# Turning the rows of an attention input by transposing transfers instead of on TensorE

## The chip, the cores and the metric

The kernel runs on one core of one Trainium2 chip. The metric is the device time of one execution in microseconds, the median over the runs shown. A profile of one execution stands beside it; all rows quoted here are from that profile or from queries of its trace. TensorE multiplies matrices out of SBUF into PSUM, ScalarE (ACT) and VectorE (DVE) do element-wise work, GpSimd (POOL) issues the indirect transfers here, and SyncE (SP) issues the plain ones. Each engine works through its own instructions in order.

## The reference

The input has 16 batches of 512 features by 1024 tokens, and a mask of zeros and ones by token. One attention layer of 8 heads is added to the input; queries, keys and values are the same projection:

```python
xt = jnp.transpose(x, (0, 2, 1))                       # x: (16, 512, 1024)
q = xt @ Wq.T
qh = q.reshape(B, T, NH, dk).transpose(0, 2, 1, 3)     # NH = 8, dk = 64
scores = scale * jnp.einsum('bhqd,bhkd->bhqk', qh, qh)
cmask = mask[:, None, None, :]
rmask = mask[:, None, :, None]
logits = (scores * cmask + (1.0 - cmask) * NEG) * rmask
attn = jax.nn.softmax(logits, axis=-1)
ctx = jnp.einsum('bhqk,bhkd->bhqd', attn, qh)
out = ctx.transpose(0, 2, 1, 3).reshape(B, T, D) @ Wo.T
return x + jnp.transpose(out, (0, 2, 1))
```

About half of the tokens of a batch are masked. A masked query gets all logits zero, so its attention is the plain mean over all tokens; an unmasked query attends only to unmasked tokens.

## The kernel before, in words

The kernel keeps only the unmasked ("active") tokens of a batch: up to 544 for batches 0 to 4, 528 for 5 to 13 and 512 for 14 and 15 (`self.wide`); batches 2 to 15 are ordered by their number of active tokens. Index lists are computed on the chip, and the rows of active tokens are gathered by indirect transfers into tiles of 128 tokens by 512 features (`gather`, tag `xa`, 13 buffers; the 32 or 16 rows beyond 512 go to `xt`, one buffer).

Method `xt` (line 476) brings them into the layout that the projection wants, features on partitions: four transposes per tile on TensorE against the identity (L486), into PSUM, and then `xsplit` makes two half-precision parts of the result: ScalarE writes the rounded value times 256 to `xh` (L444), VectorE the remainder to `xl` (L445). `xh` and `xl` exist once, 4 blocks of 546 columns each; column A, behind the active tokens, takes the mean over all tokens. The mean comes from a plain load of the batch (`load_all`, tag `xm`) that ScalarE sums (L425).

`query` (L513) multiplies these by the weights, three half-precision products per block of features, for four blocks e of outputs and two halves g of the columns. `qsplit` splits the result again and spreads it over partitions by four SP transfers (`xx`, L540 to L543). `value` brings it back to tokens on partitions; `scores` (L701) forms two heads' scores for 128 keys, ScalarE takes the exponential (L705, tag `p`, 12 buffers); `attend` (L726) multiplies by the values. The remainder of the tokens beyond 512 (`i` is None, L676, L680) is packed for four heads, split by VectorE and spread by SP transfers (`pt`, L692, L693), and taken up by L730. `recip_rows` sends the reciprocals of the sums through DRAM (`rd`, L769; `rb`, L773); `norm` applies them and splits the context; `project` (L817) multiplies by the output weights, VectorE adds the input row (L822), and an indirect transfer writes the rows out (`scatter`, L901).

The masked tokens' rows get one vector per batch, the projected mean: `late` gathers them (tag `xi`, 8 buffers), `rest` adds the vector `ub` (tag `ub`, 3 buffers; L888) and writes the row out. They are handled one to three batches after their own.

The loop `run` goes over 16 batches in 18 steps. While batch b's scores are formed, a list `m` of units for batch b+1 (the transposes, queries, values) and for batch b-1 (norm, project) is worked off in proportion to given costs. At the start of `m` stand the units of `xt` for batch b+1; query e=0 follows at once. Gathers for batch b+2 come late in iteration b. Transfers on POOL are posted to two lines and issued one a step; each waits for the matmul traced before it. The engines' final orders are laid out at build time by a planner that sorts by priority and estimated readiness; `high_priority(offset=HPO)` (300) puts an instruction ahead of its place, `behind` orders instructions of one engine. A tile under a tag waits for one of its buffers to be free.

```python
m = sums + x[:2] + second + x[2:4] + (value(b, 3) if b else []) + rows + x[4:] + pk(b, 1)
```

Batch 0 and the first parts of batch 1 are worked before the loop.

Of the kernel before, what the change touches and what calls it, by code (L numbers as in the profile page):

```python
# [22 lines left out]
H = 8  # L23
DK = 64
NP = H // 2
DC = D // P
# [4 lines left out]
C = 544  # L31
CT = C - 512
CQ = C + 2
HG = H // 2
NB = TB + 1
NMIN = 384
# [10 lines left out]
class Fast:  # L47
# [91 lines left out]
    def setup2(self):  # L139
        nc, fixed = self.nc, self.fixed  # L140

        self.quad = fixed("quad", [P, HG])
        nc.vector.tensor_reduce(self.quad, self.ident.rearrange("p (r t) -> p r t", r=HG), AX.X, ALU.add)
        self.xh = fixed("xh", [P, DC, CQ], F16)
        self.xl = fixed("xl", [P, DC, CQ], F16)
        for t in (self.xh, self.xl):
            nc.gpsimd.memset(t[:, :, C + 1:], 0.0)

        self.rcol = [fixed("rcol%d" % k, [P, P]) for k in range(2)]
        self.smcol = [fixed("smcol%d" % k, [P, P]) for k in range(2)]  # L150
# [264 lines left out]
    def load_half(self, b, k, after=None):  # L415

        c, h = k // 2, k % 2
        t = self.sb([P, T // 2], F32, *((("xm", 2), ("ub", 3), ("xi", 8), ("xi", 8))[k // 2 if b < 2 else 0]))
        self.once(self.nc.sync.dma_start(out=t, in_=self.x_nat[b, c * P:(c + 1) * P, h * T // 2:(h + 1) * T // 2]), after)
        self.st[b]["xm"].append(t)  # L420

# [5 lines left out]
    def load_all(self, b, c, after=None):  # L427
# [6 lines left out]
        self.once(self.nc.sync.dma_start(out=t, in_=src), after)  # L434
        self.st[b]["xm"].append(t)

    def xsplit(self, dst, src, scaled=False):
        nc = self.nc
        with self.tc.high_priority(offset=HPO):
            if scaled:  # L440
                nc.vector.tensor_copy(self.xh[dst], src)
                self.xs = nc.vector.tensor_tensor(self.xl[dst], src, self.xh[dst], ALU.subtract).ins
            else:
                nc.scalar.activation(self.xh[dst], src, AF.Copy, scale=SX)  # L444
                self.xs = nc.vector.scalar_tensor_tensor(self.xl[dst], src, SX, self.xh[dst], ALU.mult, ALU.subtract).ins  # L445

    def range_x(self, b, c):

        nc, s = self.nc, self.st[b]
        if c == 0:  # L450
            s["top4"] = self.sb([P, DC], F32, "top4", 2)
        nc.vector.tensor_reduce(s["top4"][:, c:c + 1], self.xh[:, c, :s["A"] + 1], AX.X, ALU.max, apply_absolute_value=True)
        if c == DC - 1:
            nc.vector.tensor_reduce(self.big[:, b:b + 1], s["top4"], AX.X, ALU.max)

# [18 lines left out]
    def xt(self, b, k):  # L474

        nc, s = self.nc, self.st[b]
        A = s["A"]
        n = P if k < 4 else A - 512
        if n:
            x = s["xa"][k] if k < 4 else s["xt"]  # L480
            if b == 0:
                pt = self.ps_s.tile([P, 2, D], F32, tag="s", name="pss")[:, 0, :DC * n].rearrange("p (c n) -> p c n", c=DC)
            else:
                pt = self.pm([P, DC, n])
            for c in range(DC):
                self.pe = nc.tensor.transpose(pt[:, c, :], x[:n, c * P:(c + 1) * P], self.ident[:n, :n]).ins  # L486
            self.last_xt = self.pe
            self.xsplit((slice(None), slice(None), slice(k * P, k * P + n)), pt)
            self.last_xs = self.xs
        if k == 4:  # L490
            if b and A < self.wide[b - 1]:
                for t in (self.xh, self.xl):
                    nc.gpsimd.memset(t[:, :, A + 1:A + 2], 0.0)
            ms = self.sb([P, DC], F32, "ms", 2)
            m = s["ms2"].rearrange("p (c h) -> p c h", h=2)
            if b < 2:
                with self.behind(s["at"]):
                    nc.vector.tensor_tensor(ms, m[:, :, 0], m[:, :, 1], ALU.add)
            nc.vector.tensor_scalar(ms, ms if b < 2 else s["ms2"][:, :DC], SX / T, None, ALU.mult)
            self.xsplit((slice(None), slice(None), A), ms, True)  # L500

    def query(self, b, e, g):
# [6 lines left out]
        wh, wl = self.w["q"]  # L509
        k = 0  # L510
        for c in range(DC):
            for w, xx in ((wh, self.xh), (wh, self.xl), (wl, self.xh)):
                self.beat = nc.tensor.matmul(pq, lhsT=w[:, c, e * P:(e + 1) * P], rhs=xx[:, c, cols],  # L513
                                             start=(k == 0), stop=(k == 3 * DC - 1)).ins
                k += 1
# [145 lines left out]
    def scores(self, b, p, i):  # L661
# [8 lines left out]
        if i is None:  # L670
            pt = self.ps_s.tile([P, 2, 512], F32, tag="s", name="pss")
            for a in range(2):
                for g in range(2):
                    for r in range(HG):
# [1 line left out]
                        self.beat = nc.tensor.matmul(pt[r * CT:(r + 1) * CT, g, :CH], lhsT=xx[:, 2 * k, 512:C],  # L676
                                                     rhs=xx[:, 2 * k + a, g * CH:(g + 1) * CH],
                                                     start=(a == 0), stop=(a == 1)).ins
            t = self.sb([P, C], F32, "p", 12)[:, :A]
            nc.scalar.activation(t.rearrange("p (g c) -> p g c", g=2), pt[:, :, :CH], AF.Exp,  # L680
                                 bias=s["nm"][p][:, HG:], scale=SCALE, accum_out=s["zt"][:, p:p + 1])

# [16 lines left out]
        for a in range(2):  # L699
            for g in range(2):  # L700
                self.beat = nc.tensor.matmul(pt[:, g, :CH], lhsT=xx[:, 2 * k, i * P:(i + 1) * P],  # L701
                                             rhs=xx[:, 2 * k + a, g * CH:(g + 1) * CH],
                                             start=(a == 0), stop=(a == 1)).ins
        t = self.sb([P, C], F32, "p", 12)[:, :A]
        self.exp = [nc.scalar.activation(t.rearrange("p (g c) -> p g c", g=2), pt[:, :, :CH], AF.Exp,  # L705
                                         bias=s["nm"][p // HG][:, p % HG:p % HG + 1], scale=SCALE,
                                         accum_out=s["z"][:, p, i:i + 1]).ins]
# [69 lines left out]
    def norm(self, b, p):  # L777
# [3 lines left out]
        o = k * CT  # L781
        if p == 0:

            s["ch"] = self.sb([P, NP, 512], F16, "ch", 2) if b < self.B - 1 else self.xh[:, :, :512]
            s["cl"] = self.sb([P, NP, 512], F16, "cl", 2) if b < self.B - 1 else self.xl[:, :, :512]
# [43 lines left out]
            self.plus(x, po)  # L829
        self.scatter(s["idx"][:, i:i + 1], x)  # L830

    def late(self, b, j, tag="xi", bufs=8):

        self.post(lambda: self.late_now(b, j, *(("xg", 1) if j == 4 else (tag, bufs))), urgent=j == 4)

# [36 lines left out]
    def spread(self, group, rows):  # L872
# [3 lines left out]
        for k, row in enumerate(rows):  # L876
            nc.sync.dma_start(out=ud[k:k + 1, :], in_=row)
        for k, o in enumerate(group):
            ub = self.st[o]["ub"] = self.sb([P, D], F32, "ub", 3)
            nc.sync.dma_start(out=ub, in_=ud[k:k + 1, :].broadcast_to([P, D]))  # L880

    def rest(self, b, j):
# [50 lines left out]
    def run(self, flag):  # L933
# [101 lines left out]
        if True:  # L1035
            for b in range(B + 1):
# [44 lines left out]
                            m.insert(k + 1 + 3 * c, (0, L(self.split, "o", c)))  # L1081
                else:

                    places = [("xi", 8), ("xa", 13)]
                    come = [[L(self.late, x, j, *places[k % 2]) for j in range(5, 9)] for k, x in enumerate(rests[b])]
                    leave = [[L(self.rest, x, j) for j in range(5, 9)] for x in rests[b]]
                    free[0] = come[0]
# [215 lines left out]
```

## Time and profile before

| | us |
|---|---|
| median of 2 runs | 1041.62 (1040.9 to 1042.35) |
| profiled execution, first to last instruction (span) | 1032.2 |
| what lies around the span (median less span) | 9.4 |
| TensorE busy | 988.2 (96%) |
| VectorE busy | 725.1 (70%) |
| ScalarE busy | 659.5 (64%) |
| GpSimd busy | 300.8 (29%) |

The profiled execution's own time outside its span isn't recorded; the sum in the prediction is made against the span. How to read the rows: a group's row has the line in the code, the engine, the operation, what is written <- what is read, the shape and count, then busy time in us and the mean ns of one, and behind the bar the idle time of the engine before these instructions with what ended it. A row of waits has who waited <- for whom, the total in us, the number of times and the longest. A row of the timeline has the start and the length in us, and in brackets the idle time before it. PE is TensorE's matmuls, PEld its weight loads, SPq and POOLq the queues that issue transfers. Matmuls are pipelined, so neighbours overlap in the rows.

### The profile page before, as it was taken

How to read it: one execution, taken by the hardware profiler on the slowest of the kernel's cores; microseconds unless marked ns; L12 is line 12 of the kernel's file. 1: busy time of each engine (PE TensorE's matmuls, PEld its weight loads, DVE VectorE, ACT ScalarE, POOL GpSimd, SP SyncE). 2: the span in 40 equal slices, each digit the busy share in tenths (PEclk: the TensorE clock that was granted, in tenths of full speed). 3: DMA queues.
4: the chain of work that ended last, by engine and by line, in shares of the span. 5: the costliest groups of instructions: out<-in, count | busy, mean ns of one | idle time of the engine just before them, and what ended most of it. 6: DMA issues, size and time to landing. Idle time of an engine off the chain costs nothing. (4 is left out here: it accounts for less than half of the span.)

```text
span 1032.2 us, 23511 instructions
## 1 busy us (share of the span) xinstructions
PE 988.2 (96%) x8455; PEld 685.0 (66%) x8455; DVE 725.1 (70%) x2410; ACT 659.5 (64%) x1702; POOL 300.8 (29%) x307
## 2 busy tenths in 40 slices
PE   7798999999999999999999999999999999999996
PEld 6576667666676766767666676767666666776563
DVE  6897668676775767877666787767777777666653
ACT  5876767557667666667667567756667667665550
POOL 3101013223311232233232333323232322325562
PEclk9999999999999999999999999999999999999999
DMA  6746546557554586575657565576565666556652
GB/s 199 231 139 183 136 134 161 183 161 206 165 142 128 150 239 172 151 209 148 190 157 227 172 169 168 163 203 185 163 210 138 192 184 184 151 142 191 185 183 95
DMA packets 78795, 177.73 MB, mean 172 GB/s; under 512 B 14688, under 2 KB 20576, under 8 KB 78672
## 3 DMA queue, kind: packets, MB, share of 16 engines
q1 hardware_dynamic: 57584, 108.40, 38.8%
q0 software_dynamic: 21088, 67.75, 20.9%
q8 instruction: 69, 1.13, 0.5%
q14 instruction: 54, 0.44, 0.1%
HBM read 91.49 MB, written 33.91 MB: 121 GB/s over the span
## 5 line engine op out<-in xcount | busy, mean ns | idle before, releaser
L705 ACT ACTIVATE p<-pss,nm 128x528 f32<-128x528 f32 (+2 forms) x512 | 359.5, 706 | 169.6 <-PE pss L701 160.0
L701 PE MATMUL pss<-xx 128*128 128x264 f16 (+2 forms) x2048 | 300.9, 276 | 6.1 <-ACT p L705 5.2
L726 PE MATMUL pav<-p,v 128*64 128x264 f32 (+2 forms) x2048 | 243.3, 390 | 0.0
L701 PEld LDWEIGHTS <-xx 128*128 128x128 f16 x2048 | 194.2, 99 | 62.4 <-issue 25.1
L726 PEld LDWEIGHTS pav<-p,v 128*64 128x64 f32 x2048 | 141.4, 137 | 85.7 <-issue 13.5
L901 POOL DMA_INDIRECT y_out<-xa,idx x68 | 73.5, 1081 | 285.4 <-PE pss L701 101.6
L513 PE MATMUL pm<-xh,wqh 128*128 128x264 f16 (+5 forms) x512 | 142.2, 278 | 4.1 <-DVE xa L822 3.4
L513 PE MATMUL pm<-xl,wqh 128*128 128x264 f16 (+5 forms) x512 | 141.6, 277 | 0.2 <-DVE xl L445 0.2
L513 PE MATMUL pm<-xh,wql 128*128 128x264 f16 (+5 forms) x512 | 141.7, 277 | 0.0
L395 POOL DMA_INDIRECT xa<-x_in,idx x68 | 68.6, 1009 | 201.7 <-PE pss L701 81.1
L513 PEld LDWEIGHTS <-wqh 128*128 128x128 f16 x1024 | 98.3, 99 | 24.0 <-issue 7.5
L705 ACT ACTIVATION_READ_ACCUMULATOR p<-pss,nm 128x1 f32 x512 | 103.9, 203 | 0.0
L901 POOL DMA_INDIRECT y_out<-xi,idx x60 | 72.6, 1211 | 97.0 <-PE pss L701 26.5
L817 PE MATMUL pm<-woh,ch 128*128 128x512 f16 x240 | 91.1, 379 | 0.0
L817 PE MATMUL pm<-woh,cl 128*128 128x512 f16 x240 | 90.9, 379 | 0.0
L817 PE MATMUL pm<-wol,ch 128*128 128x512 f16 x240 | 90.9, 379 | 0.0
L395 POOL DMA_INDIRECT xi<-x_in,idx x60 | 61.3, 1021 | 95.3 <-PE pss L701 31.9
L516 ACT ACTIVATE q<-pm 128x264 f32<-128x264 f32 (+5 forms) x128 | 50.2, 392 | 59.9 <-PE pm L513 59.3
L822 DVE SCALAR_TENSOR_TENSOR xa<-pm,xa 128x512 f32<-128x512 f32 x60 | 41.3, 689 | 56.4 <-PE pm L817 52.7
L817 PEld LDWEIGHTS <-ch 128*128 128x128 f16 x480 | 46.1, 98 | 44.8 <-issue 0.9
L799 DVE TENSOR_TENSOR c<-c,rb 128x528 f32<-128x528 f32 (+2 forms) x64 | 45.4, 710 | 43.0 <-DMA rb<-rd 21.3
L888 DVE TENSOR_TENSOR xi<-xi,ub 128x512 f32<-128x512 f32 (+1 forms) x60 | 40.8, 688 | 41.8 <-PE pss L701 41.2
(223 smaller groups left out, 1509.6 us busy)
## 6 DMA issues: line engine op xcount, KB each, us to landing
xx<-hl SPq DMA_DIRECT2D x224, 136.0 KB
xm<-x_nat_in SPq DMA_DIRECT2D x56, 512.0 KB
rb<-rd SPq DMA_DIRECT2D x72, 132.0 KB
rb<-rd SPq DMA_DIRECT2D x40, 136.0 KB
pt<-c SPq DMA_DIRECT2D x36, 132.0 KB
pt<-p SPq DMA_DIRECT2D x36, 132.0 KB
ub<-ud SPq DMA_DIRECT2D x16, 256.0 KB
xx<-hl SPq DMA_DIRECT2D x32, 128.0 KB
```

Of the source, the lines that this page charges most:

```text
L395: dma = self.nc.gpsimd.indirect_dma_start(out=tile[:n], out_offset=None, in_=self.x, in_offset=bass.IndirectOffsetOnAxis(ap=idx, axis=0))
L513: self.beat = nc.tensor.matmul(pq, lhsT=w[:, c, e * P:(e + 1) * P], rhs=xx[:, c, cols], start=(k == 0), stop=(k == 3 * DC - 1)).ins
L516: nc.scalar.activation(s["q"][:, e, cols], pq, AF.Copy, scale=1.0 / (SX * SW))
L701: self.beat = nc.tensor.matmul(pt[:, g, :CH], lhsT=xx[:, 2 * k, i * P:(i + 1) * P], rhs=xx[:, 2 * k + a, g * CH:(g + 1) * CH], start=(a == ...
L705: self.exp = [nc.scalar.activation(t.rearrange("p (g c) -> p g c", g=2), pt[:, :, :CH], AF.Exp, bias=s["nm"][p // HG][:, p % HG:p % HG + 1 ...
L726: mm = nc.tensor.matmul(s["pav"][k * DK:(k + 1) * DK, g, :CH], lhsT=s["v"][p][:, i, k * DK:(k + 1) * DK], rhs=ps[k][:, cols], start=(i == ...
L799: self.once(nc.vector.tensor_tensor(c[:, :A], c[:, :A], s["rb"][p], ALU.mult), self.beat if p < 3 else None)
L817: nc.tensor.matmul(po[:cols.stop - cols.start], lhsT=a[:, e, cols], rhs=w[:, e, :], start=(e == 0 and k == 0), stop=(e == DC - 1 and k == 2))
L822: self.nc.vector.scalar_tensor_tensor(x, po, 1.0 / (SX * SW), x, ALU.mult, ALU.add)
L888: self.once(self.nc.vector.tensor_tensor(x[:n], x[:n], s["ub"][:n], ALU.add), self.beat)
L901: dma = self.nc.gpsimd.indirect_dma_start(out=self.out, out_offset=bass.IndirectOffsetOnAxis(ap=idx, axis=0), in_=x, in_offset=None)
```

## The change

For batches 1 to 15, `xt` no longer transposes on TensorE. ScalarE and VectorE split the gathered rows where they lie, tokens on partitions, into a tile `xs` (one buffer) that holds the upper and the lower halves side by side, 1024 numbers per token; one SP transfer with `transpose=True` turns these into the eight blocks of `xhl`. `xhl` takes the place of `xh` and `xl`: one tile with the four upper and four lower blocks, 560 columns each, two buffers, so that a batch's can be filled while the one before is still read. Batch 0 goes on as before. One column behind the mean is set to zero for each batch by one memset on POOL, in place of the earlier two at the start and where the width changes. The readers of `xh` and `xl` (`range_x`, `query`, the last batch's context in `norm`) use the batch's own views. Three tags get fewer buffers: `p` 12 to 11, `xi` 8 to 4, `ub` 3 to 2; the first batches' loads use the same tags.

```diff
+CX = 560
...
-        self.xh = fixed("xh", [P, DC, CQ], F16)
-        self.xl = fixed("xl", [P, DC, CQ], F16)
-        for t in (self.xh, self.xl):
-            nc.gpsimd.memset(t[:, :, C + 1:], 0.0)
+        self.inputs(0)
...
-        t = self.sb([P, T // 2], F32, *((("xm", 2), ("ub", 3), ("xi", 8), ("xi", 8))[k // 2 if b < 2 else 0]))
+        t = self.sb([P, T // 2], F32, *((("xm", 2), ("ub", 2), ("xi", 4), ("xi", 4))[k // 2 if b < 2 else 0]))
...
+    def inputs(self, b):
+        t = self.xhl = self.sb([P, 2 * DC, CX], F16, "xhl", 2)
+        self.xh, self.xl = t[:, :DC], t[:, DC:]
+        self.st[b]["x"] = self.xh, self.xl
+        a = self.wide[b]
+        self.nc.gpsimd.memset(t[:, :, a + 1:a + 2], 0.0)
...
         n = P if k < 4 else A - 512
-        if n:
+        if b and k == 0:
+            self.inputs(b)
+        if n and b:
+            x = s["xa"][k] if k < 4 else s["xt"]
+            t = self.sb([P, 2, D], F16, "xs", 1)
+            with self.tc.high_priority(offset=HPO):
+                nc.scalar.activation(t[:n, 0], x[:n], AF.Copy, scale=SX)
+                self.last_xs = nc.vector.scalar_tensor_tensor(t[:n, 1], x[:n], SX, t[:n, 0], ALU.mult, ALU.subtract).ins
+                self.pe = self.last_xt = nc.sync.dma_start(out=self.xhl[:, :, k * P:k * P + n], in_=t[:n].rearrange("p k d -> p (k d)"),
+                                                           transpose=True).ins
+        elif n:
...
-            if b and A < self.wide[b - 1]:
-                for t in (self.xh, self.xl):
-                    nc.gpsimd.memset(t[:, :, A + 1:A + 2], 0.0)
...
-            for w, xx in ((wh, self.xh), (wh, self.xl), (wl, self.xh)):
+            xh, xl = s["x"]
+            for w, xx in ((wh, xh), (wh, xl), (wl, xh)):
...
-            t = self.sb([P, C], F32, "p", 12)[:, :A]
+            t = self.sb([P, C], F32, "p", 11)[:, :A]
...
-    def late(self, b, j, tag="xi", bufs=8):
+    def late(self, b, j, tag="xi", bufs=4):
...
-            ub = self.st[o]["ub"] = self.sb([P, D], F32, "ub", 3)
+            ub = self.st[o]["ub"] = self.sb([P, D], F32, "ub", 2)
...
-                    places = [("xi", 8), ("xa", 13)]
+                    places = [("xi", 4), ("xa", 13)]
```

More of the change, by code (lines that the diff above doesn't have):

```diff
@@ L451, in range_x @@
             s["top4"] = self.sb([P, DC], F32, "top4", 2)
-        nc.vector.tensor_reduce(s["top4"][:, c:c + 1], self.xh[:, c, :s["A"] + 1], AX.X, ALU.max, apply_absolute_value=True)
+        nc.vector.tensor_reduce(s["top4"][:, c:c + 1], s["x"][0][:, c, :s["A"] + 1], AX.X, ALU.max, apply_absolute_value=True)
         if c == DC - 1:
@@ L703, in scores @@
                                              start=(a == 0), stop=(a == 1)).ins
-        t = self.sb([P, C], F32, "p", 12)[:, :A]
+        t = self.sb([P, C], F32, "p", 11)[:, :A]
         self.exp = [nc.scalar.activation(t.rearrange("p (g c) -> p g c", g=2), pt[:, :, :CH], AF.Exp,
@@ L782, in norm @@
         if p == 0:
-            s["ch"] = self.sb([P, NP, 512], F16, "ch", 2) if b < self.B - 1 else self.xh[:, :, :512]
-            s["cl"] = self.sb([P, NP, 512], F16, "cl", 2) if b < self.B - 1 else self.xl[:, :, :512]
+            s["ch"] = self.sb([P, NP, 512], F16, "ch", 2) if b < self.B - 1 else s["x"][0][:, :, :512]
+            s["cl"] = self.sb([P, NP, 512], F16, "cl", 2) if b < self.B - 1 else s["x"][1][:, :, :512]
             if self.kept[b] > 512:
```

## The prediction

> **What bounds the kernel now.** I read the page's head first, to see which engine is full, then the busy time of the engines in single stretches, to see whether it is full throughout. Columns of the second kind: stretch and its length, then busy time (and instructions) of PE, PEld, DVE, ACT and POOL, granted clock, DMA share, GB/s.
>
> ```profile
> span 1032.2 us, 23511 instructions
> PE 988.2 (96%) x8455; PEld 685.0 (66%) x8455; DVE 725.1 (70%) x2410; ACT 659.5 (64%) x1702; POOL 300.8 (29%) x307
> q1 hardware_dynamic: 57584, 108.40, 38.8%
> ...
> 0.00:60.00 60.00, 47.03 (x435) 37.11 (x436) 47.46 (x150) 41.20 (x110) 12.44 (x33) 0.94 0.70 208
> 480.00:540.00 60.00, 58.66 (x514) 41.22 (x514) 43.10 (x145) 40.14 (x106) 18.49 (x17) 1.00 0.63 179
> 540.00:600.00 60.00, 58.31 (x493) 40.05 (x493) 43.06 (x143) 39.54 (x103) 18.56 (x18) 1.00 0.67 194
> ```
>
> A batch takes about 60 us. In the middle of the program TensorE is busy 58.66 and 58.31 us of 60, at full granted clock; DVE and ScalarE have some 17 and 20 us to spare. Only the first 60 us hold a real hole, 13 us. The page's chain of what ended last holds only the closing wait and says nothing, so I went to the list of waits, which says who starves whom.
>
> ```profile
> ACT p L705 <- PE pss L701: 160.0, 102, 3.5
> ACT xh L444 <- PE pm L486: 33.3, 14, 3.1
> PE pav L730 <- DMA pt<-p: 6.0, 7, 1.8
> PE pss L701 <- ACT p L705: 5.2, 11, 0.6
> ```
>
> ScalarE's exponentials waited 160.0 us for scores; TensorE waited 5.2 us for the exponentials and 6.0 us for a transfer. So TensorE bounds every stage after the first 60 us, and its in-order queue is where a gain or a loss is read.
>
> **What leaves TensorE.** The groups of the transposes, by shape (columns: busy us, mean ns of one | idle before), and how they lie in the queue (start us, length):
>
> ```profile
> L486 PE MATMUL pm<-ident,xa 128*128 128x128 f32 x240 | 33.0, 277 | 0.0
> L486 PE MATMUL pm<-ident,xt 16*128 16x16 f32 x36 | 3.7, 213 | 0.1
> L486 PE MATMUL pm<-ident,xt 32*128 32x32 f32 x16 | 1.7, 227 | 0.2
> ...
> 532.92 1.04 PE L486 MATMUL pm<-ident,xa 128*128 128x128 f32 x8
> 533.80 0.61 PE L701 MATMUL pss<-xx 128*128 128x264 f16 x4
> ```
>
> For batches 1 to 15, 60 tiles of 128 rows (four transposes each) and 13 tails go. Their busy time is 33.0 + 3.7 + 1.7 = 38.4 us, which is the upper end. Neighbours overlap: eight begin at 532.92 and the next matmul at 533.80, so a tile of four holds the queue 0.44 us. 60 x 0.44 = 26.4 us, and with the tails' 5.4 us it is 31.8 us. I take **32 us** off, between 26 (no tails) and 38.4.
>
> **What moves between ScalarE and VectorE.** The splits now read SBUF. Nearest rows are the weights' splits, 128x512 from SBUF:
>
> ```profile
> L444 ACT ACTIVATE xh<-pm 128x512 f16<-128x512 f32 x60 | 33.0, 594 | 33.4 <-PE pm L486 33.3
> L444 ACT ACTIVATE xh<-pm 128x64 f16<-128x64 f32 x9 | 2.3, 257 | 0.1
> L180 ACT ACTIVATE woh<-xa 128x512 f16<-128x512 f32 x4 | 2.4, 674 | 0.0
> L445 DVE SCALAR_TENSOR_TENSOR xl<-pm,xh 128x512 f16<-128x512 f32 x60 | 38.8, 683 | 11.8 <-ACT xh L444 11.5
> L181 DVE SCALAR_TENSOR_TENSOR wol<-xa,woh 128x512 f16<-128x512 f32 x4 | 2.7, 683 | 0.1
> ```
>
> ScalarE: 60 x (674 - 594) = 4.8 us more, and 13 tails that now run 512 long: 13 x 0.42 = 5.4 us. VectorE: 683 against 683 for tiles, about 6 us for tails. Ten us on an engine that waited 160.0 us for TensorE are hidden by that wait; without that cover they would cost 10. The mean column is written as before, and the memset of one column per batch is on POOL, 29% busy. I count 0.
>
> **The new chain: split, turn, next split.** One half-pair buffer exists, so tile k+1 may be split only when tile k's transfer (256 KB) has landed. The trace has no transposing transfer. I bound its time from issue to landing, L, by rows of the queue it uses, and look at when the rows come and when they are needed.
>
> ```profile
> 541.44 0.31 SPq L769 DMA_DIRECT2D rd<-rr  x1
> 543.26 1.11 SPq L773 DMA_DIRECT2D rb<-rd  x2
> ...
> 522.61 0.59 SPq L693 DMA_DIRECT2D pt<-p  x1
> 527.75 0.48 PE L730 MATMUL pav<-pt,vt 128*128 128x264 f32 x2 [0.82 <-DMA pt<-p]
> ...
> 520.43 0.98 POOL L395 DMA_INDIRECT xa<-x_in,idx  x1 [0.89 <-PE pm L637]
> 532.91 0.94 POOL L395 DMA_INDIRECT xa<-x_in,idx  x1 [2.76 <-PE pss L701]
> xa<-x_in,idx POOLq DMA_INDIRECT x68, 5.4
> ...
> 542.40 0.28 PE L513 MATMUL pm<-xh,wqh 128*128 128x264 f16 x1
> 543.75 0.28 PE L513 MATMUL pm<-xh,wqh 128*128 128x266 f16 x1
> ```
>
> Low end of L: 5 KB from 541.44 to the dependent issue at 543.26, 1.8 us. Middle: a 132 KB copy issued at 522.61 released TensorE at 527.75, 5.1 us with others in the queue. High end: queue 1 took 38.8% of 16 x 1032.2 us for 57,584 packets, 111 ns each; if turning cuts 256 KB into pieces of 256 bytes (128 halves), 1024 packets on 16 engines are 64 x 0.111 = 7.1 us, and with 1.8 us of latency L is 8.9 us. I take 5.1, the row of the same queue and nearest size.
>
> The gathers go out from 520.43 to 532.91 and take 5.4 us, so rows land from 525.8 to 538.3. With L = 5.1 a link of the chain is 0.67 + 0.68 + 5.1 = 6.5 us: tiles turned at 532.3, 538.8, 545.3 and 551.8, the short tail near 556. The first query now begins at 542.40 (it needs tiles 0 to 2), the second at 543.75 (it needs all). They come 3 and 12 us late. What covers that on TensorE is the projection, ready soon after:
>
> ```profile
> 496.14 0.39 PE L817 MATMUL pm<-woh,ch 128*128 128x512 f16 x1
> 498.52 0.38 PE L817 MATMUL pm<-woh,cl 128*128 128x512 f16 x1
> 491.15 3.78 PE L726 MATMUL pav<-p,v 128*64 128x264 f32 x32
> 492.18 0.69 ACT L705 ACTIVATE p<-pss,nm 128x528 f32<-128x528 f32 x1
> 495.53 0.70 ACT L705 ACTIVATE p<-pss,nm 128x528 f32<-128x528 f32 x1 [2.56 <-PE pss L701]
> ```
>
> One projection is 496.14 to 498.90, 2.6 us of queue, four a batch are 10.4 us, and a group of attention matmuls 3.78 us. If the planned order puts these ahead, the 12 us are covered; without cover they would cost 14 x 12 = 168 us. I charge 0.2 us a batch, **3 us**.
>
> **Leaner buffers.** p, 12 to 11: the last exponential of a pair (492.18) now waits until the attention group begun at 491.15 has freed its first quarter (0.95 us, so 492.1): nothing, and 2.56 us of ScalarE idleness stand behind it; at worst 0.5 us x 64 groups. xi, 8 to 4: in the middle rows leave before the next come. Near the end they do not:
>
> ```profile
> 913.75 0.97 POOL L395 DMA_INDIRECT xi<-x_in,idx  x1 [2.49 <-PE pm L513]
> 938.20 1.09 POOL L395 DMA_INDIRECT xi<-x_in,idx  x1 [0.30 <-DVE c L800]
> 942.58 1.32 POOL L901 DMA_INDIRECT y_out<-xi,idx  x1 [3.30 <-PE pm L569]
> 1027.19 0.96 POOL L901 DMA_INDIRECT y_out<-xa,idx  x1 [0.30 <-issue]
> ```
>
> Eight gathers go out from 913.75 to 938.20 before the first row leaves at 942.58; four of them must now move behind leaving rows, up to 29 us later, but the kernel ends with xa rows at 1027.19, some 80 us on: 0, at worst 10 us. ub, 3 to 2, is needed one batch at a time: 0. The first batches' loads wait for fewer buffers in the hole of the first 60 us: **2 us**, 0 to 8.
>
> **SP's queue** takes five more issues a batch, 5 x 0.59 = 3 us if they are like others, in front of copies that TensorE already waited 6.0 us for. Were each of the 28 tail copies 0.6 us later, that is 17 us; I take 0 to 17, and **1 us**.
>
> **Sum.** -32 + 3 + 2 + 1 = -26 us. The profiled execution spans 1032.2 us, the median of the runs shown is 1041.62, so 9.4 us lie around the span: 1006 us of span, **1016 us** of time. Own range: 26 to 38.4 off and 0 to 13 added, 1003 to 1026.
>
> **Rivals.** *ScalarE stands at the single buffer (slower).* The next split sits in ScalarE's in-order queue among the exponentials. Place: four waits in each of 15 batches. Price: where a transfer lands d us after the moment for which the order was laid out, ScalarE stands d, and TensorE, two score tiles ahead, follows after ScalarE's usual slack, 160.0 / 102 = 1.57 us a time. Net -26 + 60 x (d - 1.57): break-even at d = 2.0, slower by 2% from 2.4 us; at d = 3 it is +60, **1101 us**. For: with DMA at 63% busy, landing times scatter (1.8 to 5.1 us in the rows above). Against: TensorE waited only 6.0 us for the tail copies, so the order allows for transfers well. Chance 0.30.
>
> *Queries late, TensorE waits (no change).* With L between 5 and 9 us the cover is short by some 2 us a batch: 14 x 1.9 = 27 us, and it is **1042 us**. For: rows land at 538.3, only 5 us before the second query. Against: 10.4 us of projections. Chance 0.25.
>
> *The turn is as slow as the high end.* L = 8.9 makes a link 10.3 us, the fourth tile lands at 567 and the tail near 572, 28 us late. Cover 10.4 + 2 x 3.78 = 18 us, so 10 us a batch: 1042 - 32 + 140 = **1150 us**. For: nothing in the trace shows a faster one. Against: the packets of queue 1 are mostly longer than 256 bytes, and short ones may be cheaper. Chance 0.07. [...]
>
> **Chances.** Forecast 0.38; a measurement tells no less than about 2%, 21 us, from no change. Faster (below 1021): 0.37, from the forecast's cases but its slow edge. Within 2%: 0.27, the late queries, that edge and a mild stand at the buffer. Slower: 0.36, the other two rivals. Eight times in ten the time should lie from 1003 (the forecast's best) to 1101 (a stand of d = 3); beyond lie the slow turn and longer stands. The likeliest case's own range stays 1003 to 1026.
>
> **What will show it.** Right: no L486 rows but batch 0's, TensorE's busy time near 950 us, its waits still small, and ScalarE's splits waiting little. The single buffer: a new wait of ScalarE for the turning transfer, some 60 times, and TensorE's for exponentials far over 5.2 us. Late queries: TensorE waiting at L513 for a transfer, once or twice a batch. Slow turn: the DMA share well over 0.7 and SP's issues far over 0.59 us. The forecast is wrong if TensorE's idle time grows by more than its busy time shrinks.

## The result

The change made the kernel slower by a tenth: 1149.95 us (1149.01 to 1150.9) against 1041.62, a ratio of 1.1032 with a 95% interval of 1.0988 to 1.1076. The profiled execution took 1150.9 us and spans 1149.1. First the head of the page, the rows that answer to those of before:

```profile
span 1149.1 us, 23162 instructions
PE 1010.9 (88%) x8163; PEld 673.5 (59%) x8163; DVE 731.9 (64%) x2410; ACT 664.6 (58%) x1702; POOL 305.4 (27%) x317
DMA packets 143739, 194.00 MB, mean 169 GB/s; under 512 B 79488, under 2 KB 85376, under 8 KB 143616
q1 hardware_dynamic: 122528, 124.70, 43.9%
```

The 292 transposes are gone (8455 matmuls to 8163), yet TensorE is busy longer, 1010.9 us for 988.2, and it is idle 1149.1 - 1010.9 = 138.2 us where it was idle 44.0. So the 117 us of the span are 94 us of idle time and 23 us of busy time; against the 988.2 - 38.4 = 949.8 us that were to remain, the same matmuls took 61 us longer.

### The profile page after: what moved, and what is told of

Same layout as the page of the kernel before. It is cut to its first block, busy times and chain, and to the rows that moved or that the text cites. A ratio compares the mean times of both kernels' runs of the same rounds, so it can differ in the third digit from the quotient of the medians.

```text
span 1149.1 us, 23162 instructions
## 1 busy us (share of the span) xinstructions
PE 1010.9 (88%) x8163; PEld 673.5 (59%) x8163; DVE 731.9 (64%) x2410; ACT 664.6 (58%) x1702; POOL 305.4 (27%) x317
## 5 line engine op out<-in xcount | busy, mean ns | idle before, releaser
L714 PE MATMUL pss<-xx 128*128 128x264 f16 (+2 forms) x2048 | 315.4, 286 | 42.8 <-ACT p L718 32.1
L714 PEld LDWEIGHTS <-xx 128*128 128x128 f16 x2048 | 200.2, 102 | 119.6 <-issue 77.2
L739 PE MATMUL pav<-p,v 128*64 128x264 f32 (+2 forms) x2048 | 256.7, 406 | 0.0
L526 PE MATMUL pm<-xhl,wqh 128*128 128x264 f16 (+5 forms) x1024 | 190.8, 287 | 31.0 <-DVE nm L652 16.3
L739 PEld LDWEIGHTS pav<-p,v 128*64 128x64 f32 x2048 | 147.0, 143 | 95.5 <-issue 27.0
L526 PE MATMUL pm<-xhl,wql 128*128 128x264 f16 (+5 forms) x512 | 147.0, 287 | 0.0
L526 PEld LDWEIGHTS <-wqh 128*128 128x128 f16 x1024 | 100.9, 101 | 59.8 <-issue 36.7
L491 DVE SCALAR_TENSOR_TENSOR xs<-xa,xs 128x512 f16<-128x512 f32 x60 | 41.5, 692 | 131.9 <-ACT xs L490 121.7
L490 ACT ACTIVATE xs<-xa 128x512 f16<-128x512 f32 x60 | 37.8, 629 | 146.1 <-DMA xhl<-xs 101.9
L914 POOL DMA_INDIRECT y_out<-xi,idx x60 | 69.9, 1166 | 109.5 <-PE pss L714 34.1
```

The source lines that it names most:

```text
L490: nc.scalar.activation(t[:n, 0], x[:n], AF.Copy, scale=SX)
L491: self.last_xs = nc.vector.scalar_tensor_tensor(t[:n, 1], x[:n], SX, t[:n, 0], ALU.mult, ALU.subtract).ins
L739: mm = nc.tensor.matmul(s["pav"][k * DK:(k + 1) * DK, g, :CH], lhsT=s["v"][p][:, i, k * DK:(k + 1) * DK], rhs=ps[k][:, cols], start=(i == ...
L914: dma = self.nc.gpsimd.indirect_dma_start(out=self.out, out_offset=bass.IndirectOffsetOnAxis(ap=idx, axis=0), in_=x, in_offset=None)
```

## The profile after, and where the time went

The same two stretches as before (columns as in the prediction):

```profile
480.00:540.00 60.00, 52.80 (x428) 35.39 (x427) 39.03 (x128) 35.66 (x93) 17.47 (x17) 0.91 0.67 179
540.00:600.00 60.00, 54.89 (x449) 35.47 (x446) 38.39 (x123) 37.26 (x95) 18.27 (x17) 0.94 0.58 163
```

TensorE is no longer full in the middle (52.80 and 54.89 us of 60, before 58.66 and 58.31), and the granted clock is 0.91 and 0.94 where it was 1.00. VectorE and ScalarE have even more room than before. Nothing is full: something stands. The list of waits (who waited <- for whom, us in total, times, longest) says who:

```profile
DVE xs L491 <- ACT xs L490: 137.1, 55, 5.1
ACT xs L490 <- DMA xhl<-xs: 114.7, 47, 5.0
ACT xs L490 <- DMA xa<-x_in,idx: 42.6, 15, 4.0
PE pss L714 <- ACT p L718: 32.1, 40, 3.0
PE pm L607 <- ACT qt L594: 20.1, 9, 3.0
PE pm L526 <- DVE nm L652: 16.3, 7, 7.7
PE pm L526 <- DMA xhl<-xs: 9.4, 11, 2.0
```

ScalarE stands 114.7 us ahead of a split until the turning transfer of the tile before has landed, and 42.6 us until gathered rows have; VectorE stands behind it. TensorE now waits 32.1 us for exponentials (5.2 before), 20.1 us for the copies `qt` (no row before) and 16.3 us for `nm` of VectorE (0.4 before). All of its stops that ended with ScalarE add up to 84.4 us in the full list, to 7.5 before: most of the 94 us of new idle time. The last row is what the prediction watched: the queries wait for their transfer only 9.4 us.

One such stand, and what it does, in rows picked from the timelines of the three engines and SP (start, length, in brackets the idle time before and what ended it; the rows between them are left out):

```profile
578.03 0.21 ACT L718 ACTIVATION_READ_ACCUMULATOR p<-pss,nm 128x1 f32 x1
581.85 0.63 ACT L490 ACTIVATE xs<-xa 128x512 f16<-128x512 f32 x1 [3.61 <-DMA xhl<-xs]
583.34 0.42 ACT L594 COPY qt<-q 128x256 f32<-128x256 f32 x1
583.81 0.44 PE L607 MATMUL pm<-ident,qt 128*128 128x128 f32 x2 [2.24 <-ACT qt L594]
587.45 1.45 SPq L492 DMA_TRANSPOSE xhl<-xs  x1
588.40 5.06 PE L739 MATMUL pav<-p,v 128*64 128x264 f32 x32
591.50 0.63 ACT L490 ACTIVATE xs<-xa 128x512 f16<-128x512 f32 x1 [2.05 <-DMA xhl<-xs]
592.88 1.23 SPq L492 DMA_TRANSPOSE xhl<-xs  x1
597.84 1.13 SPq L492 DMA_TRANSPOSE xhl<-xs  x1
601.22 0.59 PE L526 MATMUL pm<-xhl,wqh 128*128 128x266 f16 x2 [1.49 <-DMA xhl<-xs]
602.93 0.43 PE L526 MATMUL pm<-xhl,wql 128*128 128x266 f16 x1
606.74 0.28 PE L526 MATMUL pm<-xhl,wql 128*128 128x266 f16 x1
```

ScalarE has nothing in hand from 578.24 to 581.85 because the next instruction of its order is a split that waits for a transfer. The copy `qt`, due behind it, ends at 583.76, and TensorE, through with its projections, stands 2.24 us for it. The second loss follows: the group of 32 attention matmuls at 588.40, 3.78 us before, takes 5.06, and the query matmuls at 601.22 to 603.6, after a stop of 1.49 us, take 0.43 us where they take 0.28 a little later. The granted clock (the column behind POOL) in steps of 2 us around these stops:

```profile
582.00:584.00 2.00, 0.19 (x2) 0.19 (x3) 1.37 (x4) 2.00 (x5) 0.00 (x0) 1.00 0.00 0
584.00:586.00 2.00, 1.75 (x10) 1.07 (x10) 1.79 (x4) 1.13 (x4) 0.19 (x1) 0.55 0.62 137
586.00:588.00 2.00, 0.98 (x5) 0.54 (x4) 1.24 (x4) 1.93 (x6) 0.75 (x1) 0.50 0.74 209
588.00:590.00 2.00, 2.00 (x11) 0.99 (x10) 1.93 (x7) 1.44 (x5) 0.75 (x1) 0.50 0.97 247
...
602.00:604.00 2.00, 2.00 (x11) 1.43 (x9) 1.03 (x2) 0.00 (x0) 0.00 (x0) 0.50 1.01 233
606.00:608.00 2.00, 2.00 (x21) 1.73 (x19) 2.00 (x14) 0.71 (x4) 0.59 (x1) 1.00 0.77 231
```

After these stops, of 2.24 us to 583.81 and of 1.49 us to 601.22, the clock is 0.50 for 6.8 and 3.4 us (read in steps of 0.1 us: from 584.2 to 591.0 and from 601.3 to 604.7) and then 1.00 again. So a stop goes with two losses in these rows: the idle time itself, and longer matmuls behind it.

## The experiments

Ratios are to the kernel before in the same job, since before took 1032 to 1044 us from job to job. Every kernel's order is laid out anew by the planner, so differences of half a per cent are not read, and a difference holds whatever the new order does as well.

**The leaner buffers** (done alone on the kernel before) and, next to them, the kernel after with TensorE's transposes put back, which leaves the buffers and the double tile.

```diff
...
-            t = self.sb([P, C], F32, "p", 12)[:, :A]
+            t = self.sb([P, C], F32, "p", 11)[:, :A]
...
-    def late(self, b, j, tag="xi", bufs=8):
+    def late(self, b, j, tag="xi", bufs=4):
...
-            ub = self.st[o]["ub"] = self.sb([P, D], F32, "ub", 3)
+            ub = self.st[o]["ub"] = self.sb([P, D], F32, "ub", 2)
...
```

> The kernel before with the three leaner tags alone (p 11, xi 4, ub 2), transposes still on TensorE. If the loss comes from the single split buffer or from the turning transfers, this stays at 1042 us, within 10 us. If the leaner buffers carry it, it rises towards 1100 us or more, with new waits of ScalarE for p or of GpSimd for xi.

```diff
-        if n and b:
+        if n and b > 99:
```

> The changed kernel with TensorE's transposes put back: leaner buffers and the double tile, but no split on tokens and no turning transfer. Transfers or the single buffer as cause: 1042 us, within 10 us. Anything in the double tile or the leaner buffers as cause: well above 1060 us.

Measured 1.0081 (1.0053 to 1.0108) and 1.0100 (1.0068 to 1.0132). The room costs about 1%, some 10 us, before anything is turned in it; not nothing, but a tenth of the loss.

**One suspect at a time: the single buffer, ScalarE, the priority.** Three `xs` buffers (room from `xm`):

```diff
...
-        t = self.sb([P, T], F32, "xm", 2)
+        t = self.sb([P, T], F32, "xm", 1)
...
-            t = self.sb([P, 2, D], F16, "xs", 1)
+            t = self.sb([P, 2, D], F16, "xs", 3)
```

> The changed kernel with three split buffers in place of one; room for them comes from one xm buffer in place of two. Single buffer as cause: ScalarE's waits for the turning transfer fall from 114.7 us to under 30 us, TensorE's granted clock comes back from 0.94 to 0.98 or more, and the time falls to 1030 to 1070 us. Late turned tiles as cause (rows land late, transfers take their time whatever the buffers): ScalarE's waits fall too, but TensorE now waits for xhl by 60 us or more, and the time stays above 1120 us.

Measured 1.0899 (1.0868 to 1.0931). In the list of waits the wait for the transfer is gone; the same engine stands at the same line for the rows instead:

```profile
ACT xs L490 <- DMA xa<-x_in,idx: 92.5, 45, 5.4
PE pss L714 <- ACT p L718: 24.9, 23, 5.1
```

Both halves on VectorE, so that ScalarE takes no part in the split:

```diff
-                nc.scalar.activation(t[:n, 0], x[:n], AF.Copy, scale=SX)
+                nc.vector.tensor_scalar(t[:n, 0], x[:n], SX, None, ALU.mult)
```

> The changed kernel with the upper half made by VectorE in place of ScalarE; still one split buffer, so the chain of split, turn and next split is as long as before. ScalarE's place in the chain as cause: the stand of some 115 us moves to VectorE, which has 17 us a batch to spare, and the time falls to 1030 to 1090 us. Chain length as cause: the time stays within 20 us of 1150 us.

Measured 1.1060 (1.1027 to 1.1094): VectorE takes over both waits, and TensorE now stands for what VectorE prepares (the spread query halves, `xx`):

```profile
DVE xs L490 <- DMA xhl<-xs: 105.3, 48, 4.2
DVE xs L490 <- DMA xa<-x_in,idx: 40.4, 15, 3.9
PE pm L582 <- DMA xx<-hl: 42.1, 24, 6.2
```

The split without its priority:

```diff
-            with self.tc.high_priority(offset=HPO):
+            with ExitStack():
```

> The changed kernel with the split and the turning transfer at their own place in the order instead of 300 places ahead; one split buffer. If the engines stand because the split is put ahead of exponentials before its rows or its buffer are there, ScalarE's waits for rows and transfer fall under 60 us together and the time falls to 1060 to 1110 us. If the chain is simply too long for its place, it only starts later: TensorE waits for turned tiles instead and the time stays at 1150 us or rises.

Measured 1.1223 (1.1192 to 1.1254). ScalarE's waits fall little (82.4 us for transfers, 43.3 us for rows), and TensorE's wait for exponentials grows to 45.4. None of the three is the cause by itself.

**Taking a wait away.** A constant tile is split in place of the rows, with the transfers as they are:

```diff
-                nc.scalar.activation(t[:n, 0], x[:n], AF.Copy, scale=SX)
...
+                still = self.ident[:n].unsqueeze(1).broadcast_to([n, 4, P])
+                nc.scalar.activation(t[:n, 0].rearrange("p (a c) -> p a c", a=4), still, AF.Copy, scale=SX)
...
```

> The changed kernel with a constant tile split in place of the gathered rows; gathers, splits and turning transfers all still run, one split buffer (left out: the true rows as input of the projection; the closing flag is set to pass). The chain no longer hangs on the gathers and can start a batch ahead. If the chain only starts too late: 1000 to 1040 us. If the turning transfers themselves, their length, their traffic or their issues on SP, carry the loss: above 1100 us, ScalarE still waiting some 100 us for them.

Measured 1.0451 (1.0410 to 1.0491): without the wait for rows about half of the loss is left, and ScalarE's wait for the transfer (86.5 us in 41) stays. The same with three `xs` buffers:

> The constant tile is split, all turning transfers run, with three split buffers (one xm buffer) (left out: the true rows as input; the closing flag is set to pass). If the transfers only hurt by holding the one buffer: 1010 to 1035 us and ScalarE's waits for them under 20 us. If their traffic or their place in SP's queue hurts: above 1060 us, with TensorE waiting for xx, rb or pt.

Measured 1.0577 (1.0542 to 1.0613), not better; ScalarE still waits 84.8 us in 44 for transfers. In this kernel some of the transfers wait themselves, for the queries (L527 here) that still read the tile to be filled:

```profile
SPq L493 <- PE pm L527: 35.7, 12, 3.8
```

With one `xs` buffer it is 35.8 us in 13; in the kernel after, whose splits come later, no transfer waits so. So part of the stand in these two kernels is of another kind than the one that they were to show.

Without transfers (the queries read zeros), with real rows and with the constant tile:

> The changed kernel without the turning transfers: the rows are split as in the change, but the double tile is only set to zero once a batch and the queries read that; the closing flag is set to pass (left out: the turn itself, so the output is not the reference's). It keeps the split's wait for the gathered rows. If the turning transfers carry the loss: 1005 to 1025 us, the gain that TensorE's 32 to 38 us promise. If the wait for late rows carries it: above 1080 us, with ScalarE still waiting some 40 us or more for the gathers.

> The last two cuts together: a constant tile is split and nothing is turned; the queries read zeros (left out: the true rows and the turn; the closing flag is set to pass). If the waits for late rows and for the transfer are the whole loss: 1005 to 1025 us, which is the time before less the 32 us of transposes plus the 9 us that the leaner buffers cost. If the splits themselves or the order of the rest carry part of it: above 1050 us.

Measured 1.0663 (1.0624 to 1.0702) and 1.0310 (1.0246 to 1.0373). In both the zeros are written by a memset of the whole tile in every batch, and in the second of them GpSimd is busy 361.0 us and VectorE 769.4, where it is 305.4 and 731.9 in the kernel after. So they don't decompose the loss; the four kernels below do without that memset.

**Another place in the order.** Three tries to give the chain more room: queries later in the round, with gathers and projections ahead of them; each split pinned behind the exponential before it; and both. The first and the last have three `xs` buffers as above; the first leaves out the priority, too. The diff has the pin and the line of the last that matters most.

```diff
-            with self.tc.high_priority(offset=HPO):
+            with self.behind(*self.exp):
...
-                    m += q(2, 1) + pk(n, 0) + P_(2) + (take if b else []) + tp(n, 0) + q(3, 0) + bt(n, 0)
...
+                    m += hot + tail + x[3:4] + P_(0) + x[4:] + index + rest + P_(1) + take + q(0, 0) + q(0, 1) + q(1, 0) + q(1, 1) + tc(0) + v(0) + tv(0) + rng[:2]
...
```

> Three split buffers (one xm buffer), no hoist, and another order of the units of an iteration: one projection ahead of the first query, the index list and the gathers of the batch after next earlier, so that rows land long before their split and the turned tiles before their queries. If late rows and late tiles carry the loss: 1000 to 1050 us, with ScalarE's waits for rows and transfers under 30 us. If the transfers cost otherwise (traffic, SP's queue), the time stays above 1100 us.

> The changed kernel, order of units and one split buffer as they are, but the split is put on ScalarE behind the exponential that is traced just ahead of it, and nothing is hoisted. If the loss comes from splits that the planner puts where it believes rows have landed: ScalarE's waits for rows fall from 42.6 to under 15 us, the time to 1080 to 1125 us, the waits for the one buffer staying. If the chain is too long for its place: waits move to TensorE at the queries, and the time stays at 1150 us or above.

> Pinned as in the run before, three split buffers (one xm buffer), the tiles of a batch spread over the first steps, and one projection and a half ahead of the first query; gathers of the batch after next ahead of the queries. If waits for rows and transfers are the cause, both fall under 30 us together and the time is 1015 to 1060 us. If rows cannot land earlier because their buffers come free late, ScalarE still waits some 60 us for gathers and the time stays above 1100 us.

Measured 1.1131 (1.1077 to 1.1184), 1.1396 (1.1363 to 1.1429) and 1.1148 (1.1097 to 1.1198). In the first ScalarE still waits 71.8 us for rows, in 37 times. In the pinned kernel it no longer waits for rows, but the queries come late, and that is the second rival's wait:

```profile
PE pss L714 <- ACT p L718: 64.6, 73, 4.6
PE pm L526 <- DMA xhl<-xs: 31.6, 16, 3.1
```

Pinned and with queries later, ScalarE's waits for rows and transfers fall to 5.3 us, and TensorE waits at the values instead (L582 for `xx`, 31.9 us in 20). Put early, ScalarE and VectorE stand; put late, TensorE does.

**From nothing up.** Four kernels build the path from none. In the first three the query reads one tile of zeros.

```diff
...
-                nc.scalar.activation(t[:n, 0], x[:n], AF.Copy, scale=SX)
-                self.last_xs = nc.vector.scalar_tensor_tensor(t[:n, 1], x[:n], SX, t[:n, 0], ALU.mult, ALU.subtract).ins
-                self.pe = self.last_xt = nc.sync.dma_start(out=self.xhl[:, :, k * P:k * P + n], in_=t[:n].rearrange("p k d -> p (k d)"),
-                                                           transpose=True).ins
+            pass
...
```

> Left out for every later batch: the split, the turning transfer and the transposes; the query matmuls read one fixed tile of zeros, and the closing flag is set to a pass. This is the kernel after with the whole new path at no price and no wait. If the saving of the prediction (TensorE's 32 us) is there to be had once the rows need no preparing, the leaner buffers (1.008 by themselves) leave 0.97 to 0.985 of before, about 1005 to 1020 us. If instead the saved TensorE time can't be turned into time at all, because ScalarE, VectorE or the order of the units bounds an iteration as closely as TensorE does, 1.00 or more.

> As the kernel without the whole path, but ScalarE and VectorE each do the split of a constant tile, at the place and in the order of the kernel after; no rows are waited for, no transfer is issued, the query reads the fixed tile (no dependence on the split). The work alone (about 0.63 us of ScalarE and 0.69 us of VectorE a tile, 73 tiles, less what the transposes' evictions took). If the engines hide it as the prediction said, at most 0.01 above the kernel without the path. If ScalarE or VectorE are bounds of an iteration, 0.02 to 0.04 above it.

> As the one before, but the split reads the real gathered rows, so ScalarE waits for them; no transfer is issued. If the early place of the split ahead of the landing gathers is what costs (the theory that ScalarE and VectorE stand for gathers), 0.03 to 0.06 above the kernel that splits a constant tile, with ScalarE's wait for the gathers near 50 us. If the wait for the turning transfer is the price, at most 0.01 above.

> No split: the 73 transfers turn one fixed tile of zeros, from the place and the queue of the kernel after, and the query waits for its transfer as there. If the transfers hurt by what they are (SP's 1.24 us of issue each, 64,944 more packets beside the gathers), 0.03 or more above the kernel without the path. If they hurt only through the split that stands before and after them, at most 0.01 above.

| kernel | ratio (95%) | TensorE busy, idle | clock |
|---|---|---|---|
| no path | 0.9830 (0.9780 to 0.9879) | 959.6, 56.8 | 0.991 |
| split of a constant | 0.9892 (0.9863 to 0.9921) | 963.6, 66.6 | 0.986 |
| transfers alone | 0.9928 (0.9902 to 0.9953) | 966.5, 69.5 | 0.984 |
| split of the real rows, no transfers | 1.0377 (1.0328 to 1.0427) | 979.5, 97.7 | 0.973 |
| split of a constant, transfers | 1.0451 (1.0410 to 1.0491) | 975.2, 103.3 | 0.977 |
| all (the kernel after) | 1.1032 (1.0988 to 1.1076) | 1010.9, 138.2 | 0.944 |

Busy, idle and clock are those of one profiled execution; that of "transfers alone" was the slowest of its ten, 1037.67 us for a median of 1032.89. All six have the same 8163 matmuls. TensorE's stops that ended with ScalarE, added up as above, are 16.5, 19.0 and 15.2 us in the first three kernels, 40.2 and 42.4 in the next two, and 84.4 in the last. Zeros don't run faster in them: an attention matmul of the first lasts 389 ns, as in the kernel before. Its rows, with those of the kernel before below:

```profile
L736 PE MATMUL pav<-p,v 128*64 128x264 f32 x1152 | 136.1, 389 | 0.0
```

```profile
L726 PE MATMUL pav<-p,v 128*64 128x264 f32 x1152 | 136.1, 389 | 0.0
```

Read from the top, in us of 1041.6: the buffers cost 10 (1.0100), and taking the transposes and the splits behind them away gives 28 (1.0100 to 0.9830). The split's work costs 6 (0.9892 - 0.9830), the transfers by themselves 10 (0.9928 - 0.9830), so these 16 us would have left 0.999. The wait for rows adds 1.0377 - 0.9892 = 0.0485, 50 us. A transfer between two splits adds 1.0451 - 0.9830 - 0.0062 - 0.0098 = 0.046, 48 us. All together is 1.0935 of the measured 1.1032; the last 10 us are the two waits acting on each other, or the order. By the intervals each of these differences is uncertain by some 6 us, so that the 6 are hardly more than nothing, and the ratios come from four jobs. The 48 hold the transfers that waited for the queries. The other way round, in the kernel with real rows and no transfers, the transfers add 1.1032 - 1.0377 = 0.0655, 68 us, of which 10 are theirs alone; so 58 us by that reading. The first of these waits, in the kernel with real rows and no transfers:

```profile
ACT xs L492 <- DMA xa<-x_in,idx: 82.6, 40, 4.5
```

So neither operation is dear. What is dear is that an engine that feeds TensorE stands, in order, for two things that land late. In the kernel before the rows were waited for by TensorE, which had other work until late; its only wait for these tiles was this:

```profile
PE pss L486 <- DMA xa<-x_in,idx: 2.5, 1, 2.5
```

**On an engine that feeds nothing.** The split on GpSimd, in three operations, two `xs` buffers:

```diff
+                nc.gpsimd.tensor_scalar(g[:n], x[:n], SX, None, ALU.mult)
+                nc.gpsimd.tensor_copy(t[:n, 0], g[:n])
+                self.last_xs = nc.gpsimd.tensor_tensor(t[:n, 1], g[:n], t[:n, 0], ALU.subtract).ins
```

> The split moves to GpSimd, as three operations (scale to f32, halve to f16, take the rest), with two xs buffers and one xm buffer; rows, transfers and queries are those of the kernel after. If the loss is ScalarE and VectorE standing in order for gathers and transfers ahead of TensorE's work, their xs waits go, GpSimd (27% busy) stands in their place, and the kernel comes down to the sum of the single parts, 0.98 to 1.02 of before. If it is the length of the way from rows to turned tile, which this makes longer by the three operations (0.2 us for a 128x128 memset there, so an estimate of 0.8 us or more each), or if GpSimd's standing holds up the gathers and scatters that it issues, TensorE waits at the query for the transfer or the rows and the time stays above 1.06.

Measured 1.2193 (1.2133 to 1.2253), the worst of all. First two waits, then SP's timeline (start, length; no idle times are given for it):

```profile
PE pm L584 <- DMA xx<-hl: 121.6, 27, 6.8
POOL xp L491 <- DMA xa<-x_in,idx: 100.1, 41, 5.2
```

```profile
559.51 0.48 SPq L555 DMA_DIRECT2D xx<-hl  x1
560.04 0.61 SPq L556 DMA_DIRECT2D xx<-hl  x1
560.70 0.59 SPq L557 DMA_DIRECT2D xx<-hl  x1
561.34 0.67 SPq L558 DMA_DIRECT2D xx<-hl  x1
...
574.57 0.48 SPq L555 DMA_DIRECT2D xx<-hl  x1
...
581.48 1.24 SPq L494 DMA_TRANSPOSE xhl<-xs  x1
...
583.41 0.59 SPq L556 DMA_DIRECT2D xx<-hl  x1
585.50 1.23 SPq L494 DMA_TRANSPOSE xhl<-xs  x1
586.78 0.59 SPq L557 DMA_DIRECT2D xx<-hl  x1
587.41 0.60 SPq L558 DMA_DIRECT2D xx<-hl  x1
```

GpSimd stands 100.1 us for the rows in ScalarE's place, and its three operations make a split 3.4 us long (their groups' means are 1529, 701 and 1185 ns). SP, in order too, can issue a turning transfer only when the split is done, and what stands behind it waits along. The four spreading transfers of one query, which begin within 1.8 us at 559.51, take 12.8 us from 574.57, with turning transfers between them, and TensorE stands 121.6 us for such transfers at the values. Freeing ScalarE and VectorE doesn't help when the way to the query gets longer and SP stands in turn. The 0.98 to 1.02 that the theory gave did not come: the stand moved to two other queues and was not removed, so this run doesn't test ScalarE's part by itself.

**Rows earlier.** Index lists and gathers one projected tile earlier in the round, two more buffers for rows, one fewer for `xm`:

```diff
-                    m += rng[:2] + tc(0) + tail + P_(0) + v(0) + tv(0) + rest + P_(1) + (hot if b else []) + rng[2:] + q(2, 0) + v(1) + (index if b else [])
-                    m += q(2, 1) + pk(n, 0) + P_(2) + (take if b else []) + tp(n, 0) + q(3, 0) + bt(n, 0)
+                    m += rng[:2] + tc(0) + (hot if b else []) + tail + P_(0) + v(0) + tv(0) + rest + (index if b else []) + P_(1) + (take if b else []) + rng[2:] + q(2, 0) + v(1)
+                    m += q(2, 1) + pk(n, 0) + P_(2) + tp(n, 0) + q(3, 0) + bt(n, 0)
```

> The hottest rows and the list of indices of the batch after next are made, and its gathers posted, one projected tile earlier in the round; two more buffers for the rows hold them (15 for 13, room from one xm buffer less); one xs buffer, all else as in the kernel after. If the way from landed rows to turned tile is too long for its place (the theory), the rows' part of it goes: ScalarE's wait for the gathers from 43 us to near nothing, the wait for the transfer before stays, and the kernel comes to 1.03 to 1.07 of before, near the 1.045 of the kernel that splits a constant tile. If the splits are put as early as the rows allow and only move with them, the waits and the 1.09 to 1.11 stay. If the earlier list work collides with TensorE's projections, above 1.11.

Measured 1.0748 (1.0686 to 1.0810), just above the 1.03 to 1.07 that were expected and the best of the kernels that turn real rows by transfers:

```profile
ACT xs L490 <- DMA xhl<-xs: 100.8, 39, 5.1
ACT xs L490 <- DMA xa<-x_in,idx: 23.7, 15, 2.5
```

ScalarE's wait for rows falls from 42.6 to 23.7 us and not to nothing, that for transfers only to 100.8; TensorE is busy 983.5 us at a granted clock of 0.971. The place of the gathers is part of the cause; that it also took an `xm` buffer stays mixed into the number. No version here beats the kernel before. One that issues the gathers a whole round ahead, with the room for them, wasn't tried.

## Why the prediction was wrong

- **TensorE's 32 us** were there: between the kernel without the path and the one with the transposes and the leaner buffers its busy time differs by 992.6 - 959.6 = 33.0 us, and the time by 28 us.
- **The splits' ten us at nothing** held nearly: the whole split, 37 us of ScalarE's busy time (668.1 - 630.8), costs about 6 us of time, and the durations held (629 ns on ScalarE for an assumed 674, 692 on VectorE for 683).

```profile
L490 ACT ACTIVATE xs<-xa 128x512 f16<-128x512 f32 x60 | 37.8, 629 | 146.1 <-DMA xhl<-xs 101.9 <-DMA xa<-x_in,idx 42.6 <-DVE c L812 1.6
L491 DVE SCALAR_TENSOR_TENSOR xs<-xa,xs 128x512 f16<-128x512 f32 x60 | 41.5, 692 | 131.9 <-ACT xs L490 121.7 <-DMA xa<-x_in,idx 5.6 <-DMA xhl<-xs 2.6
```

- **Leaner buffers at 0** (plus 2 us of the start): about 10 us. **SP's queue at 1 us**, bounds 0 to 17: the transfers alone cost about 10.
- **L, 5.1 us, was too long rather than too short.** The transfer issued at 587.45 let the next split begin at 591.50, 4.05 us; the one issued at 597.84 let TensorE begin at 601.22, 3.4 us. Over the waits of ScalarE for a transfer it is 2.8 to 5.7 us in 46 of 47 (8.6 in the one that ended at 46.59), 4.2 in the middle. The slow turn (the third rival) fell with it: of its signs SP's longer issues came (1.24 us in the middle), the DMA share over 0.7 did not (0.67 and 0.58). The link was 5.4 us in the rows above (587.45 to 592.88), where 6.5 was assumed.
- **The step that failed is "The new chain: split, turn, next split"**, where it says "I charge 0.2 us a batch, 3 us". I asked when the last tile comes to TensorE and what covers it there, and the trace bears that out (9.4 us of waits at the query in the whole program). I didn't ask it of each link, though each begins on ScalarE, passes VectorE and SP, and stands in all three ahead of work that TensorE needs. Against the 3 us charged, those waits cost 50 us for the rows and 48 to 58 for the transfers, as differences between kernels. That "ScalarE waited 160.0 us for TensorE" hides busy time, nearly all of the split; it hides a stand only if the stand falls into the same moments.
- **The first rival had the engine and the sign**: ScalarE at the split, predicted about 60 times, measured 47 for transfers and 15 for rows. Its place was too narrow. With three buffers the wait goes over to the rows, and the rows' wait was in no part of the prediction: it looked up when rows land (525.8 to 538.3) and never asked who would stand for them. Its price was too small too: by its formula 60 x (114.7 / 47 - 1.57) - 26 is +26 us, and 108 were measured.
- **The clock was in no term.** The 8163 matmuls take 959.6 us in the kernel without the path and 1010.9 after, 51 us, beside 81 us more idle time (138.2 - 56.8). In the rows the slow matmuls stand behind stops; that the stops cause them was not tried by a run of its own.
- **Late queries** (the second rival) came when splits were pinned: 31.6 us at the query, 1.1396.
- **The range's slow edge** doesn't follow from its own terms: 26 off and 13 added to 1041.62 are 1029, not 1026. Nothing hangs on it.

## What to carry to other kernels

When work leaves the full engine for a chain over others, price the chain at every in-order queue that it passes: for each link, what does the instruction wait for, and what stands behind it that the full engine will want? A wait for a gather that was nearly free on an engine with other work ahead (2.5 us on TensorE before) was not free on a half-idle engine that feeds the full one (ScalarE, 58% busy in the kernel after), nor was a wait for a transfer: here 82.6 us of ScalarE's waits for rows went with 50 us of time, 86.5 us for transfers with 48. And a stop of TensorE is to be priced with the slower matmuls after it, here 51 us beside 81.

## What the runs showed of the hardware

The granted clock fell to half after these short stops. After 2.24 us (to 583.81) it is 0.50 in the stretches from 586 to 590, with a second stop of 1.01 us between. After 1.49 us (to 601.22) it is 0.50 from 602 to 604 and 1.00 again from 606; TensorE had been busy 1.33 of the 2 us before 600. In steps of 0.1 us the clock falls at 584.2 and 601.3 and is 1.00 again from 591.0 and 604.7, 3.6 and 3.5 us after the last listed stop ahead of it ended (at 587.43 and 601.22).

By the share of queue 1 the turning transfers were cheap for the engines that carry them. The queue held 0.439 x 16 x 1149.1 - 0.388 x 16 x 1032.2 = 1663 us more of engine time for 64,944 more packets of about 250 bytes. If the other packets took as long as before, these took 26 ns each, an estimate (30 by the same sum in the kernel with the transfers alone), a quarter of the 111 ns that the queue's packets took before. So 1024 of them on 16 engines would be 1.6 us of the 4.2 of a transfer. Their issue held SP 1.13 to 1.45 us in the rows above; the four copies of `xx` between them (585.85 to 589.58) held it 0.54 to 0.59 us each.
